# A graph layer on one core: gather tiles fetched row by row from SP and ACT, the last groups placed at once, and a place for every x chunk

## The chip, the cores and the metric

The kernel runs on one core of one Trainium2 chip. The time is device microseconds of that core, the median of three executions. One more execution was profiled, and all rows shown come from it. The engines are named as in the profile: PE (matmul; PEld loads its weights), DVE, ACT, POOL, and SP, which only issues transfers. A "q" behind a name (SPq, ACTq) marks what the engine's sequencer does, issuing a DMA among it.

## The reference

```python
h = jnp.maximum(_layernorm(x, axis=-1), 0.0)          # x: 12500 x 256, f32
agg = jax.ops.segment_sum(h[src], dst, num_segments=N) # 200000 edges, sorted by dst
z = (1.0 + eps_gin) * h + agg
t = jnp.dot(z, W1) + b1                                # 256 -> 512
t = jax.nn.relu(_batchnorm(t, g1, bt1))
conv_out = jnp.dot(t, W2) + b2                         # 512 -> 256
out = x + jax.nn.relu(_batchnorm(conv_out + h, g2, bt2))
```

The batch norms take mean and variance over all 12,500 nodes, so each of them is a barrier: nothing behind it can start before the last node is in.

## The kernel before

Edges are cut into 1,563 tiles of 128, and tiles into 131 groups of 12 (`GT`; the last group has 3). Nodes are cut into 25 chunks of 512 rows (the last has 212). One row of h or x is 256 f32, 1 KB.

**Gather loop** (lines 359 to 627). Its instructions stand in the order in which the program writes them; nothing is moved by the framework's scheduler. Iteration i of the loop does, for different groups:

- `gather(i + 4)`: an indirect DMA of POOL per tile (L473), which fetches 128 rows by their source numbers. The first 30 groups (`LEAD`) fetch rows of x and normalize them on ACT and DVE (`settle`); later ones fetch rows of `h_tab`, which the first 25 iterations write (`h_chunk`). Gathered tiles have five places, so `gather(i + 4)` needs `sums(i - 1)` done. Within a group the tiles are fetched from the last to the first.
- `edges(i + 1)` (L502, DVE) makes the 0/1 matrices, and `sums(i)` (L517, PE) multiplies the tiles with them, from the first tile to the last, into one PSUM tile `ps`.
- `hold(i - 2)` (L524, ACT) copies `ps` to `zs`; `put(i - 2)` (L535, PE) spreads it over the 256 columns that the group can reach; `add(i - 4)` (L546, DVE) adds it into the chunk `zc`, which `z_load` (L492, SP) fetched from `h_cols` and `z_scale` (L496, ACT) scaled.
- A chunk that has all its groups is multiplied by W1 in four slices, one slice per iteration: `slice_of` (L553, PE), then in the next iteration `take`: statistics on DVE (L564), a copy `ts` on ACT (L566) and its store to `t_tab`, issued by ACT (L567).

After the last group, the loop runs four more iterations with what is left, and all slices still queued are done there.

In every fifth group from 34 to 124 (`APART`), the first tile is not gathered by POOL. SP fetches its 128 rows one by one (`some_rows`): it loads 16 row numbers into registers (L412), then issues 16 DMAs of 1 KB (L418), two such batches per iteration, into the tile `one`, of which there are three. The semaphores of all these DMAs are the framework's, which it deals out in turn over all DMAs of SP and ACT.

**Second product** (lines 655 to 684). Per chunk: load `ti` from `t_tab` (three places) and `yT` from `h_cols` (25 places), norm and relu on ACT (L672), multiply by W2 on PE (L679), add and take statistics on DVE. From here on the framework's scheduler may move a DMA ahead of others on its queue.

**Output** (lines 691 to 715). Per chunk: norm and relu on ACT (L699), transposes on PE (L705), add the chunk of x on DVE (L710), and store (L331). The chunks of x are loaded by SP (`x_rows`, L333): ten into places of their own or into gather buffers that are done (`xin`, `lands`), six into `xmore`, which lies where `ti` was, and the last nine into places whose chunk has been stored.

Of the kernel before, what the change touches and what calls it, by code (L numbers as in the profile page):

```python
# [7 lines left out]
F32 = mybir.dt.float32  # L8
I32 = mybir.dt.int32
# [6 lines left out]
P = 128  # L16
R = 4
# [6 lines left out]
LOW = 8  # L24
APART = 5
BATCH = 16
XAHEAD = 10
XMORE = 6
# [3 lines left out]
GROUP = 4  # L32
GAHEAD = 3


@with_exitstack
def kernel(
# [37 lines left out]
    left = E - full_tiles * P  # L75
    NG = -(-NTILE // GT)
    STEP = -(-N * P * GT // E)
    WIDE = P + 2 * MARGIN
# [231 lines left out]
    def fast():  # L310
# [24 lines left out]
        with ExitStack() as fs:  # L335
# [8 lines left out]
            with ExitStack() as es:  # L344
# [21 lines left out]
                def settle(v, pairs, rows, to, tag):  # L366
# [16 lines left out]
                    for c in reversed(range(rows)):  # L383
# [3 lines left out]

                by_row = range(LEAD + 4, NG - 6, APART)
                rows_i = keep.tile([len(by_row), P], I32, name="rows_i")
                nc.scalar.dma_start(  # L390
                    rows_i,
                    bass.AP(
                        tensor=src.tensor, offset=src.offset + by_row[0] * GT * P,
                        ap=[[APART * GT * P, len(by_row)], [1, P]],
                    ),
                )
                rows_b = keep.tile([len(by_row), P], I32, name="rows_b")
                nc.vector.tensor_scalar(rows_b, rows_i, float(4 * D), None, op0=OP.mult)
                h_bytes = h_tab.rearrange("n d -> (n d)").bitcast(U8)
                single, pending = {}, []  # L400

                def begin_rows(k):
                    i = by_row[k]
                    single[i] = sel.tile([P, D], F32, name="one", bufs=3)
                    pending.extend((k, b) for b in range(0, P, BATCH))

                def some_rows(count):

                    for _ in range(min(count, len(pending))):
                        k, b = pending.pop(0)  # L410
                        to = single[by_row[k]]
                        _, at = nc.values_load_multi_w_load_instructions(  # L412
                            rows_b[k : k + 1, b : b + BATCH], engines=[mybir.EngineType.SP], min_val=0,
                            max_val=(N - 1) * 4 * D,
                            skip_runtime_bounds_check_because="node numbers are below N",
                        )
                        for q, v in enumerate(at):
                            nc.sync.dma_start(  # L418
                                to[b + q : b + q + 1, :].bitcast(U8),
                                h_bytes[bass.ds(v, 4 * D)].rearrange("(o e) -> o e", o=1),  # L420
                            )

                xts, hts, pcs = {}, {}, {}
# [43 lines left out]
                def gather(i):  # L467
                    t0, n = groups[i]
                    k = i % (AHEAD + 1)
                    ga = lands[k] if k < EARLY else (gat.tile([P, GT, D], F32, name="gt"),)  # L470
                    for t in reversed(range(t0 + (i in by_row), t0 + n)):
                        rows = left if t == full_tiles else P
                        nc.gpsimd.indirect_dma_start(  # L473
                            out=slot(ga, t - t0)[:rows], out_offset=None, in_=x if i < LEAD else h_tab,
                            in_offset=bass.IndirectOffsetOnAxis(ap=srcT[:rows, t : t + 1], axis=0),
                        )
                    gathered[i] = ga
# [31 lines left out]
                def sums(i):  # L509

                    t0, n = groups[i]
                    ga, oh = gathered.pop(i), ohs.pop(i)
                    alone = single.pop(i, None)
                    ps = ps_s.tile([P, D], F32, name="ps")
                    for j in range(n):
                        rows = left if t0 + j == full_tiles else P
                        nc.tensor.matmul(  # L517
                            ps, lhsT=oh[:rows, j, :], rhs=alone if alone is not None and j == 0 else slot(ga, j)[:rows], start=(j == 0), stop=(j == n - 1)
                        )
                    summed[i] = ps  # L520
# [62 lines left out]
                for c in range(NCH):  # L583
                    k = max(first(c) + 1, c + 2)
                    loads.setdefault(k, []).append(c)
                    scales.setdefault(max(first(c) + 3, c + 3), []).append(c)
                    assert c + 1 < k <= first(c) + 4 and c < LEAD - AHEAD
                added = whole = 0
                for i in range(NG + 4):
                    before = added  # L590
                    if i + AHEAD < NG:
                        gather(i + AHEAD)
                    if i + APART + 3 in by_row:
                        begin_rows(by_row.index(i + APART + 3))
                    some_rows(2)

                    late = 4 if i < NG else 3
                    while added <= min(i - late, NG - 1):
# [4 lines left out]
                    taken = []  # L603
                    if 0 <= i - 2 < NG:
                        spots(i - 2)
                        hold(i - 2)
                    if i + 1 < NG:
                        edges(i + 1)

                    if i < NCH:  # L610
                        h_chunk(i)
                    if i + 1 < min(LEAD, NG):
# [4 lines left out]
                    if i < NG:  # L617
                        sums(i)
# [3 lines left out]
                    if 0 <= i - 2 < NG:  # L622
                        put(i - 2)
                    for c in loads.get(i, ()):
                        z_load(c)
                    while whole < NCH and last(whole) < (before if i < NG else added):
                        queue += [(whole, f) for f in range(HC)]
                        whole += 1
                    if i < NG:
                        some = queue[:1]  # L630
                    else:
                        some = queue
                    queue = queue[len(some):]
                    if i < NG:
                        for c, f in some:
                            slice_of(c, f)
                        taken = some
                    else:
                        for c, f in some:
                            slice_of(c, f)  # L640
                            take(c, f)
                assert added == NG and whole == NCH and not queue and not taken and not zc, (queue, taken, list(zc))

# [5 lines left out]

            xin = fs.enter_context(tc.tile_pool(name="xin", bufs=XAHEAD - EARLY, reuse_waits="tile"))  # L650
            xrs = []

            def x_rows(g):
                if g < NCH:
                    if XAHEAD - EARLY <= g < XAHEAD:
                        xrs.append(lands[g - XAHEAD + EARLY][1])
                    else:
                        pool = xmore if XAHEAD <= g < XAHEAD + XMORE else xin
                        xrs.append(pool.tile([P, R, D], F32, name="xr"))
                    carry(nc.sync, xrs[g], x, g, store=False)  # L660


            with tc.tile_pool(name="tin", bufs=3, side="right", reuse_waits="tile") as tin, tc.tile_pool(name="ps_y", bufs=4, space=PSUM) as ps_y:

                for k, g in enumerate([*range(NCH - 2), NCH - 1, NCH - 2]):
                    n = chunks[g][1] * R
                    ti = tin.tile([P, HC, CH], F32, name="ti")
                    nc.sync.dma_start(ti[:, :, :n], t_tab[g, :, :, :n])
                    nc.sync.dma_start(yT[g], h_cols[g, :, :, :n])
                    tT = lands[k % EARLY][0].rearrange("p a d -> p (a d)").rearrange("p (f n) -> p f n", n=CH)  # L670
# [5 lines left out]
                    for d in range(DC):  # L676
# [289 lines left out]
```

## Time and profile before

| | |
|---|---|
| median of 3 runs | 2212.31 us (2211.7 to 2213.7) |
| profiled execution | 2212.03 us, of which the span from first to last instruction is 2210.0 us |
| mean granted TensorE clock | 0.817 |
| busy: PE, PEld, DVE, ACT, POOL | 1388.4, 1005.3, 716.0, 511.3, 1463.2 us |
| DMA | 349.80 MB, mean 158 GB/s |

The page cuts the span into 40 slices of 55 us and gives each engine's busy tenths in them. The granted clock is a share of full speed. A group of instructions has its line, its engine, what it writes and reads, a count, its busy time, the mean duration in ns, and the idle time of the engine before it with what ended that idle time ("issue" is time in which the engine waited for nothing that the profile shows). A row of the timeline has start, duration, engine, line, operation, tiles and count.

### The profile page before, as it was taken

Reading aid. Unit: us, or ns where it says so; the run is one execution under the profiler, and the core shown is the slowest. Engines: PE = TensorE matmul, PEld = TensorE weight load, DVE = VectorE, ACT = ScalarE, POOL = GpSimd, SP = SyncE. Lnnn points to the kernel's source line nnn. Section 1 sums busy time; section 2 is a strip of 40 time slices with the busy share of each in tenths; the row PEclk is TensorE's granted clock in tenths of the full one; section 3 lists DMA queues with packets and bytes.
Section 4 is the critical chain, followed back from the end, with each engine's and each line's share of the span. In section 5 each row is a group of like instructions: output and inputs, shape, how many; then the busy total and the mean of one; then the engine's idle time right before and its main releaser. Section 6 shows DMA issues by size and latency. Waiting matters only on the chain.

```text
span 2210.0 us, 20247 instructions
## 1 busy us (share of the span) xinstructions
PE 1388.4 (63%) x4874; PEld 1005.3 (45%) x4874; DVE 716.0 (32%) x1093; ACT 511.3 (23%) x963; POOL 1463.2 (66%) x1556
## 2 busy tenths in 40 slices
PE   3666676764654655754765566564466366689994
PEld 2455455553443543543544454443354254444443
DVE  5566666531211221220222122211123022234445
ACT  4666666530000000000000000000001001024445
POOL 7777777777777777777777777777777777700000
PEclk9777888887877877877878887786788687889998
DMA  6676777544444444444444444444444445448639
GB/s 195 210 229 220 237 243 236 168 130 116 135 128 129 118 131 130 124 130 121 126 136 127 116 135 131 131 116 127 131 122 134 123 122 148 137 152 329 231 112 314
DMA packets 161627, 349.80 MB, mean 158 GB/s; under 512 B 32234, under 2 KB 87033, under 8 KB 158427
## 3 DMA queue, kind: packets, MB, share of 16 engines
q0 software_dynamic: 74096, 202.41, 33.0%
q1 hardware_dynamic: 59088, 106.53, 14.4%
q10 hardware_dynamic: 28314, 39.48, 5.0%
q8 instruction: 41, 0.67, 0.1%
q14 instruction: 88, 0.71, 0.1%
HBM read 284.29 MB, written 64.00 MB: 158 GB/s over the span
## 4 chain that ended last, share of the span: by engine, by line
POOL 39%; issue 18%; PE 17%; DMA 8%; SPq 7%; ACT 7%; DVE 3%; ACTq 0%; DVEq 0%; POOLq 0%
POOL gt L473 24%; POOL gta L473 9%; PE py L679 8%; PE ps L517 5%; SPq L418 5%; POOL gtb L473 5%; DMA gt<-in_x_dram,srcT 3%; PE ph L553 2%; ACT gt L384 2%; SPq L412 1%; PE pz L535 1%; ACT yT L699 1%; DVE stg L373 1%; DMA t_tab<-ts 1%; DMA gta<-in_x_dram,srcT 1%
## 5 line engine op out<-in xcount | busy, mean ns | idle before, releaser
L473 POOL DMA_INDIRECT gt<-h_tab,srcT x701 | 662.6, 945 | 213.6 <-issue 212.1
L517 PE MATMUL ps<-gt,oh 128*128 128x256 f32 x1834 | 497.1, 436 | 185.6 <-DMA gt<-h_tab,srcT 104.3
L517 PEld LDWEIGHTS ps<-gt,oh 128*128 128x128 f32 x1834 | 407.0, 224 | 290.7 <-issue 110.1
L473 POOL DMA_INDIRECT gta<-h_tab,srcT x323 | 305.3, 945 | 98.5 <-issue 96.9
L546 DVE TENSOR_TENSOR zc<-pz,zc 128x512 f32<-128x512 f32 (+8 forms) x187 | 94.5, 520 | 770.2 <-ACT zc L496 710.8
L535 PE MATMUL pz<-at,zs 128*128 128x256 f32 x524 | 152.7, 418 | 286.4 <-ACT zs L524 286.4
L517 PE MATMUL ps<-gta,oh 128*128 128x256 f32 x838 | 241.7, 452 | 135.6 <-DMA gta<-h_tab,srcT 73.0
L517 PEld LDWEIGHTS ps<-gta,oh 128*128 128x128 f32 x838 | 192.7, 234 | 197.5 <-issue 91.2
L473 POOL DMA_INDIRECT gt<-in_x_dram,srcT x216 | 204.1, 945 | 65.8 <-issue 61.8
L535 PEld LDWEIGHTS pz<-at,zs 128*128 128x128 f32 x524 | 104.5, 207 | 308.7 <-ACT zs L524 295.3
L502 DVE TENSOR_TENSOR oh<-col,dstT 128x1536 f32<-128x1536 f32 x131 | 227.5, 1737 | 0.0
L553 PE MATMUL ph<-zc,w1s 128*128 128x512 f32 (+1 forms) x400 | 207.5, 649 | 11.6 <-DVE hc L461 10.9
L564 DVE BATCH_NORM_STATS2 st<-ph 128x6 f32<-128x512 f32 (+1 forms) x100 | 68.2, 682 | 452.0 <-PE ph L553 451.9
L566 ACT COPY ts<-ph 128x512 f32<-128x512 f32 (+1 forms) x100 | 57.4, 574 | 675.0 <-DVE st L564 675.0
L496 ACT ACTIVATE zc<-zc,gin 128x1024 f32<-128x1024 f32 (+1 forms) x25 | 28.1, 1124 | 672.4 <-DMA zc<-h_cols 672.4
L473 POOL DMA_INDIRECT gtb<-h_tab,srcT x160 | 151.2, 945 | 48.8 <-issue 47.8
L679 PE MATMUL py<-gta,w2s 128*128 128x512 f32 (+1 forms) x400 | 169.6, 587 | 3.7 <-ACT gta L672 3.7
L553 PEld LDWEIGHTS ph<-zc,w1s 128*128 128x128 f32 x400 | 85.9, 217 | 80.2 <-issue 56.2
L679 PEld LDWEIGHTS py<-gta,w2s 128*128 128x128 f32 x400 | 76.3, 191 | 96.5 <-issue 76.6
L384 ACT ACTIVATE gt<-gt,nbg,rsg 128x256 f32<-128x256 f32 x216 | 108.1, 586 | 9.0 <-DVE nbg L382 8.5
L517 PE MATMUL ps<-one,oh 128*128 128x256 f32 x38 | 17.4, 551 | 146.1 <-DMA one<-h_tab 146.1
L672 ACT ACTIVATE gta<-ti,of,sc 128x512 f32<-128x512 f32 (+1 forms) x100 | 79.6, 802 | 82.9 <-PE py L679 78.3
(100 smaller groups left out, 1052.6 us busy)
## 6 DMA issues: line engine op xcount, KB each, us to landing
one<-h_tab SPq DMA_DIRECT2D x2432, 1.0 KB
t_tab<-ts ACTq DMA_DIRECT2D x96, 256.0 KB
ti<-t_tab SPq DMA_DIRECT2D x24, 1024.0 KB
xt<-in_x_dram SPq DMA_DIRECT2D x24, 512.0 KB
h_tab<-ht ACTq DMA_DIRECT2D x24, 512.0 KB
h_cols<-hc SPq DMA_DIRECT2D x24, 512.0 KB
zc<-h_cols SPq DMA_DIRECT2D x24, 512.0 KB
yT<-h_cols SPq DMA_DIRECT2D x24, 512.0 KB
```

The lines of the kernel that those rows point to most:

```text
L384: nc.scalar.activation(slot(to, c), slot(v, c), AF.Relu, bias=nb[:, c : c + 1], scale=rs[:, c : c + 1])
L418: nc.sync.dma_start(to[b + q : b + q + 1, :].bitcast(U8), h_bytes[bass.ds(v, 4 * D)].rearrange("(o e) -> o e", o=1),)
L473: nc.gpsimd.indirect_dma_start(out=slot(ga, t - t0)[:rows], out_offset=None, in_=x if i < LEAD else h_tab, in_offset=bass.IndirectOffsetOn ...
L502: nc.vector.tensor_tensor(ohs[i][:, :n, :], col[:, :P].unsqueeze(1).to_broadcast([P, n, P]), dstT[:, t0 : t0 + n].unsqueeze(2).to_broadcas ...
L517: nc.tensor.matmul(ps, lhsT=oh[:rows, j, :], rhs=alone if alone is not None and j == 0 else slot(ga, j)[:rows], start=(j == 0), stop=(j == ...
L535: nc.tensor.matmul(pz[:, d, :], lhsT=zs[:, d * P : (d + 1) * P], rhs=at, start=True, stop=True)
L546: nc.vector.tensor_add(side, pz[:, :, a - lo : b - lo], side)
L553: nc.tensor.matmul(ph[:, :n], lhsT=w1s[:, d, f * P : (f + 1) * P], rhs=zc[c][:, d, :n], start=(d == 0), stop=(d == DC - 1),)
L564: nc.vector.bn_stats(st1[:, f, c, :], ph[:, :n])
L566: nc.scalar.copy(ts[:, :n], ph[:, :n])
L672: nc.scalar.activation(tT[:, f, :n], ti[:, f, :n], AF.Relu, bias=of1[:, f : f + 1], scale=sc1[:, f : f + 1],)
L679: nc.tensor.matmul(py[:, :n], lhsT=w2s[:, f, d * P : (d + 1) * P], rhs=tT[:, f, :n], start=(f == 0), stop=(f == HC - 1),)
```

## The change

- SP's rows now make up 26 tiles and ACT issues the rows of 19 more. A class `Fetcher` does it for both: of every 15 groups SP serves 4 (`SP_PACE`; tile 0 of the group), and of every 5 groups ACT serves 1 (`ACT_PACE`; tile 1). Row numbers are loaded into registers 32 at a time (`LOADS`). They are fetched for each tile by a small DMA of its own on SP in iterations 19 and 20.
- Each such tile has a semaphore allocated by the kernel. Its 128 DMAs add to it, the framework's semaphores leave them out, and PE waits for all of them before the matmul of that tile. In the group's sum these tiles come last.
- The last five groups (`CLOSE`) and what follows have a loop of their own: `hold`, `put` and `add` of a group stand right behind its sums, every finished chunk is multiplied by W1 at once, and the sums take the tiles in the order in which they were gathered.
- Every chunk of x has a place that no store must free: 8 in `xin`, 5 and the rest of the last chunk in buffers that the gather loop is done with (`lands`, `dstT`, `srcT`, `w1s`), loaded behind the third chunk of the second product; 6 in `xmore` and 5 in `lands` and `w2s`, loaded at its end.

```diff
-APART = 5
-BATCH = 16
-XAHEAD = 10
+LOADS = 32
+SP_PACE = (15, 4)
+ACT_PACE = (5, 1)
+XIN = 8
 XMORE = 6
+CLOSE = 5
...
+                class Fetcher:
+                    def __init__(self, eng, kind, pace, begin, end, slot, tag):
...
+                        while begin + 2 + -(-(count + 1) * over // self.per) < end:
+                            count += 1
+                        self.groups = [begin + 2 + -(-(k + 1) * over // self.per) for k in range(count)]
...
+                    def step(self, i):
+                        upto = min((i + 1 - self.begin) * P * self.per // self.over, len(self.groups) * P)
+                        upto -= upto % LOADS
+                        while self.sent < upto:
+                            k, b = divmod(self.sent, P)
+                            self.fetch(k, b, LOADS)
+                            self.sent += LOADS
+                    def fetch(self, k, b, n):
+                        g = self.groups[k]
+                        if b == 0:
+                            self.tiles[g] = sel.tile([P, D], F32, name="one_" + self.tag, bufs=3)
+                            self.sems[g] = tc.alloc_semaphore(f"rows_{self.tag}{k}")
                         _, at = nc.values_load_multi_w_load_instructions(
-                            rows_b[k : k + 1, b : b + BATCH], engines=[mybir.EngineType.SP], min_val=0,
+                            self.at[k : k + 1, b : b + n], engines=[self.kind], min_val=0,
...
                         for q, v in enumerate(at):
-                            nc.sync.dma_start(
-                                to[b + q : b + q + 1, :].bitcast(U8),
+                            d = self.eng.dma_start(
+                                self.tiles[g][b + q : b + q + 1, :].bitcast(U8),
                                 h_bytes[bass.ds(v, 4 * D)].rearrange("(o e) -> o e", o=1),
                             )
+                            d.then_inc(self.sems[g], 16)
+                            tc.no_tile_sem_insts.add(d.ins.name)
+                            tc.add_to_no_dep_group(f"{self.tag}{g}", d.ins)
+                    def use(self, g):
+                        wait = nc.tensor.wait_ge(self.sems.pop(g), 16 * P)
+                        tc.declare_fence(wait.ins, group=f"{self.tag}{g}")
+                        return self.tiles.pop(g)
+                fetchers = [
+                    Fetcher(nc.sync, mybir.EngineType.SP, SP_PACE, LEAD - AHEAD + 1, NG - 1, 0, "s"),
+                    Fetcher(nc.scalar, mybir.EngineType.Activation, ACT_PACE, LEAD - AHEAD + 1, NG - CLOSE, 1, "a"),
+                ]
...
-                    for j in range(n):
+                    order = list(range(n)) if i < NG - CLOSE else list(reversed(range(n)))
+                    own = alone(i)
+                    order.sort(key=lambda j: j in own)
+                    for j in order:
...
+                for i in range(NG - CLOSE, NG + 1):
+                    if i + AHEAD < NG:
+                        gather(i + AHEAD)
+                    fetchers[0].step(i)
...
+                    while near < i:
+                        hold(near)
+                        while added < near - 1:
+                            add(added)
+                            added += 1
+                        put(near)
+                        near += 1
+                    while added < near:
+                        add(added)
+                        added += 1
+                    while whole < NCH and last(whole) < added:
+                        queue += [(whole, f) for f in range(HC)]
+                        whole += 1
+                    for c, f in queue:
+                        slice_of(c, f)
+                        take(c, f)
+                    queue = []
                     if i < NG:
+                        sums(i)
...
-                for g in range(XAHEAD):
-                    x_rows(g)
+                behind = [lands[k][1] for k in range(EARLY)]
+                behind += [rows_in(dstT), rows_in(srcT.bitcast(F32)), rows_in(w1s.rearrange("p a b -> p (a b)"))]
+                with tc.issue_after(begun):
+                    x_rows([(g, xin.tile([P, R, D], F32, name="xr")) for g in range(XIN)])
+                    x_rows(enumerate(behind, XIN))
+                    x_rows([(NCH - 1, rows_in(dstT, R * D, len(parts[NCH - 1])))])
...
-                for g in range(XAHEAD, XAHEAD + XMORE):
-                    x_rows(g)
+                got = len(xrs) - 1
+                x_rows([(g, xmore.tile([P, R, D], F32, name="xr")) for g in range(got, got + XMORE)])
+                last = [lands[k][0][:, c : c + R, :] for k in reversed(range(EARLY)) for c in range(0, LOW, R)]
+                last += [rows_in(w2s.rearrange("p a b -> p (a b)"))]
+                x_rows(enumerate(last, got + XMORE))
...
                     carry(nc.sync, xt, out, g, store=True)
-                    if g >= 3:
-                        x_rows(g - 3 + XAHEAD + XMORE)
```

More of the change, by code (lines that the diff above doesn't have):

```diff
@@ L625, in fast @@
                         z_load(c)
-                    while whole < NCH and last(whole) < (before if i < NG else added):
+                    while last(whole) < before:
                         queue += [(whole, f) for f in range(HC)]
                         whole += 1
-                    if i < NG:
[L630 to L633, printed above, removed]
-                    if i < NG:
[L635 to L641, printed above, removed]
@@ L642, in fast @@
[L642 removed]
+                    taken = queue[:1]
+                    queue = queue[1:]
+                    for c, f in taken:
+                        slice_of(c, f)
+                near = NG - CLOSE - 2
+                for c, f in taken:
+                    take(c, f)
+                for i in range(near, NG - CLOSE):
+                    spots(i)
+                for i in range(NG - CLOSE, NG + 1):
+                    if i + AHEAD < NG:
+                        gather(i + AHEAD)
+                    fetchers[0].step(i)
+                    if i < NG:
+                        spots(i)
+                    if i + 1 < NG:
+                        edges(i + 1)
+                    for c in scales.get(i, ()):
+                        z_scale(c)
+                    while near < i:
[12 more added lines that the diff above has]
+                    for c, f in queue:
+                        slice_of(c, f)
+                        take(c, f)
+                    queue = []
+                    if i < NG:
+                        sums(i)
@@ L644, in fast @@
+                assert added == near == NG and whole == NCH and not zc, list(zc)
             sc1, of1 = norm(keep, st1, mv1, HC, g1c, bt1c, b1c, "1")
```

101 lines of the change are left out of this document (49 added, 52 removed).

## The prediction

> **What bounds the kernel now.** I read the page first, then the busy times by stretch, then the waits, and last single rows of the instructions by line, of the chain and of the timeline. From the page:
>
> ```profile
> span 2210.0 us, 20247 instructions
> ...
> POOL 7777777777777777777777777777777777700000
> ...
> L473 POOL DMA_INDIRECT gt<-h_tab,srcT x701 | 662.6, 945 | 213.6 <-issue 212.1
> ```
>
> POOL works at one level until about 1935 us and then stops. The row of L473 says at what pace: (662.6 + 213.6) / 701 = 1.250 us for each indirect gather, 0.945 busy and 0.305 of its own issue. Of the 213.6 us idle before these gathers, 212.1 are that issue: no buffer, no late engine and no transfer holds POOL up. The stretches (us; then busy us and count of PE, PEld, DVE, ACT, POOL; TensorE clock, DMA share, GB/s) show the stages:
>
> ```profile
> 1000.00:1500.00 500.00, 290.37 (x1026) 219.54 (x1024) 106.26 (x138) 33.21 (x64) 378.10 (x401) 0.80 0.45 127
> ...
> 1935.00:1977.00 42.00, 32.38 (x91) 20.14 (x92) 13.86 (x30) 8.47 (x18) 1.51 (x2) 0.86 0.40 137
> 1977.00:2147.00 170.00, 169.43 (x400) 76.13 (x399) 67.96 (x100) 78.50 (x99) 0.00 (x0) 0.99 0.65 230
> 2147.00:2210.00 63.00, 28.29 (x196) 22.96 (x196) 32.48 (x35) 35.18 (x51) 0.00 (x0) 0.78 0.83 282
> ```
>
> So there are four: the gather loop, bound by POOL's count of gathers while ACT is busy 7% and DVE 21%; a tail of 40 us after the last gather; the second product, where PE works through; and the output, where PE, DVE and ACT are half idle and the DMA engines are not.
>
> **Gather loop: what goes.** Before, 19 of the 1,563 tiles are fetched by SP; after, 26 by SP and 19 by ACT. The pace formula gives that: SP's tiles serve groups 33, 37, 41 and on to 127, ACT's 34, 39 and on to 124. POOL thus issues 26 gathers fewer: 26 x 1.250 = **32.5 us**, all of it on the path. Its last gather ends at 1936.8 us now (below), and at 1904.3 then.
>
> **What the sequencers take on.** The two issue rows and the loads of addresses (min/median/max ns), and two loads of the chain that are four batches apart:
>
> ```profile
> L412 SPq TENSOR_LOAD <-rows_b x152: 1160/1248/1509, 423.8 to 1859.0; - x152
> L418 SPq DMA_DIRECT2D one<-h_tab x2432: 221/228/323, 425.5 to 1868.0; - x188
> L931 SPq TENSOR_LOAD <-flag x1: 476/476/476, 25.5 to 25.5; - x1
> L567 ACTq DMA_DIRECT2D t_tab<-ts x100: 325/326/357, 200.8 to 1974.8; - x100
> ...
> 537.33 1.23 SPq L412
> ...
> 563.77 1.24 SPq L412
> ```
>
> Four batches of 16 rows took 563.77 - 537.33 = 26.44 us, 6.61 each; less one load, 5.37 for 16 rows: 0.336 us per row, with the register move and now and then an instruction fetch. A load of 32 addresses is not in the trace. One address cost 0.476 and 16 cost 1.248; the straight line gives 2.07, and two loads of 16 give 2.50. I take 2.07. A tile is then 128 x 0.336 + 4 x 2.07 = 51.3 us (53.0 at the other end).
>
> SP starts at 423.8 us. Its last tile serves group 127, behind which POOL issues 12 + 12 + 3 = 27 gathers, so the tile is wanted at about 1904.3 - 27 x 1.25 = 1870. That leaves (1870 - 424) / 26 = 55.6 us a tile: SP keeps up, with 8% to spare, provided that it doesn't wait. Today it does:
>
> ```profile
> SPq L418 <- DMA t_tab<-ts: 422.8, 70, 23.6
> ...
> PE ps L517 <- DMA one<-h_tab: 146.1, 10, 24.1
> ```
>
> A row DMA of SP waits for a store that ACT issues; the DMAs share a few of the framework's semaphores in turn, so a row must wait until the store which had that semaphore has landed. With a semaphore of its own per tile, a row takes none of these, and the 422.8 us go. What is late next on SP is only the reuse of three buffers, which is what the pace is for. Behind a waiting row stand h_cols loads (`z_load`), on which ACT's scaling and DVE's adds depend; they come earlier, not later. PE's 146.1 us of waiting for rows cost POOL nothing now: group i + 4 only needs group i - 1 summed, some three groups (43 us) of cover. I count them at zero.
>
> ACT has no rows in the trace. In five groups, 5 x 11.55 x 1.25 = 72.2 us, it must issue one tile: 51.3 us at SP's price, and 51.3 + 128 x 0.098 = 63.8 if a row costs as much more as ACT's own large store (326 ns against 228). Its work of now is 33.21 us in 500, 1.0 per group, and a 0.33 us issue: 6.5. Sum 57.8 to 70.3, below 72.2 at both ends; I take the lower, since it is the same kind of DMA. Queued behind its 32 rows (12.8 us) are the `ts` copies, `zs` copies and `zc` scaling, for which PE's `put` and DVE's `add` wait; they come a group late at most, inside the same cover. The 45 address loads on SP (45 x 0.336 = 15 us, groups 19 and 20), two small DVE operations and 45 waits on PE lie beside the gathers of those groups, which wait for none of it; without that cover they would cost the 15 us once.
>
> **Early placing.** The end of the loop, from the chain and the timeline:
>
> ```profile
> 1932.16 3.02 DMA gt<-h_tab,srcT
> ...
> 1935.87 0.95 POOL L473 DMA_INDIRECT gta<-h_tab,srcT  x1 [0.31 <-issue]
> ...
> 1953.96 10.44 PE L553 MATMUL ph<-zc,w1s 128*128 128x512 f32 x20
> ...
> 1966.15 0.37 ACT L524 COPY zs<-ps 128x256 f32<-128x256 f32 x1 [0.40 <-ACT ts L566]
> ...
> 1976.80 0.70 PE L679 MATMUL py<-gta,w2s 128*128 128x512 f32 x1 [3.71 <-ACT gta L672]
> ```
>
> POOL ends at 1936.8 and the second product begins at 1976.8: 40.0 us. Between lie sums that begin with the tile gathered last, a backlog of slices (20 matmuls, 10.4 us), and group 130's placing. After, group i is placed right behind its sums, finished chunks are multiplied at once, and the last five groups sum the first-gathered tile first. What must follow POOL's end is the landing, 3.0; the last sums, about 2 (PE comes out of chunk 23's slices and group 129 at about that time); and the stretch from `zs` to `py`, 1976.80 - 1966.15 = 10.7. That is 15.7: **24.3 us saved**, at best 26. If chunk 23's slices still stand in the way, 15 us come back and 10 are saved. I take 24.3, since PE is busy 58% before it.
>
> **Places for all x chunks.**
>
> ```profile
> 1976.80 169.64 PE py L679 x400
> ...
> 2137.63 3.96 SPq L333 DMA_DIRECT2D xr<-in_x_dram  x6
> ...
> 2149.90 34.89 ACT L699 ACTIVATE yT<-yT,of,sc 128x512 f32<-128x512 f32 x50 [0.82 <-DVE of L287]
> ...
> 2185.26 1.23 DVE L710 TENSOR_TENSOR xr<-po,xr 128x1024 f32<-128x1024 f32 x1 [0.50 <-DMA out_dram<-xr]
> 2193.35 1.93 SPq L333 DMA_DIRECT2D xr<-in_x_dram  x2
> 2195.38 7.53 SPq L331 DMA_DIRECT2D out_dram<-xr  x7
> ...
> 2160.00:2190.00 30.00, 19.97 (x147) 15.64 (x147) 22.81 (x19) 24.78 (x36) 0.00 (x0) 0.99 1.08 369
> ```
>
> Today nine x chunks are loaded between the stores, each into a place that a store must free; the last is asked for at 2193.35, when ACT has been done for 8.6 us. At 369 GB/s the engines are full. After, 14 chunks come during the second product (230 GB/s, so there is room) and 11 at its end, 5.6 MB in the 17 us from 2137.6 that pass before the first output is ready. The stores alone, 12.8 MB / 369 GB/s = 34.7 us, fit ACT's 34.9. The last add then ends near 2186.5, and with the 7.1 us that now lie between the last store's issue (2202.9) and the end, plus a microsecond of backlog: 2194.6, **15.4 us saved** (8 with a backlog of another 7.5, 18 with none and a shorter drain).
>
> **The sum.** The profiled execution took 2212.03 us (span 2210.0 and 2.0 around it), the median of three is 2212.31, so nothing is to be shifted. 2212.0 - 32.5 - 24.3 - 15.4 = 2139.8; I say **2140**. The second product keeps its 169.6 us.
>
> **Rivals.**
>
> *Two issuers hold each other up* (slower). If SP's and ACT's DMAs are made by one unit that takes 0.228 us each, a row's pitch is 0.456, SP's tile 66.7 us and its last one ready at 424 + 26 x 66.7 = 2158 instead of 1870: 288 us late, 2428. It decides from 55.6 us a tile; the gain is gone at 58.3, a pitch of 0.39. Against it:
>
> ```profile
> 1360.85 1.52 SPq L418 DMA_DIRECT2D one<-h_tab  x5
> ...
> 1361.39 0.33 ACTq L567 DMA_DIRECT2D t_tab<-ts  x1
> ```
>
> Five rows took 1.52 us, their usual 0.32 each, with an ACT issue in their midst. [...] Chance 6%.
>
> *One DMA engine is full* (slower).
>
> ```profile
> q0 software_dynamic: 19202, 52.46, 38.5%
> q10 hardware_dynamic: 3600, 6.56, 3.6%
> q1 hardware_dynamic: 2546, 4.01, 2.8%
> ...
> one<-h_tab SPq DMA_DIRECT2D x844, 1.0 KB
> ...
> zc<-h_cols SPq DMA_DIRECT2D x6, 512.0 KB
> ```
>
> Between 1000 and 1500 us, SP's queue used 2.8% of 16 engines x 500 us = 224 us for 844 rows and six loads of h_cols, 3.1 MB. The latter at the price of ACT's stores (288 us for 6.56 MB) is 138, which leaves 0.10 us a row; at most it is 0.27. If all 5,760 rows went to one engine in 1,446 us, that is 40% of it (at most 107%), beside 38.5% of gathers and some 6%: 84%. It decides above 0.14 us a row; at 0.27 the loop would stretch by half, far over 2,700 us. [...] No view here names the engine. Chance 4%.
>
> *x loads stand ahead of t loads.* Thirteen whole chunks and a rest, 7.0 MB, at 369 GB/s are 19 us; two filled `ti` buffers cover 2 x 6.8. PE starts the second product 5 to 10 us short: 2148. For it: all fourteen are released at the third chunk. Against: SP serves earlier lines of the program first. 10%.
>
> *The ends give half*: 10 from placing, 8 from the places: 2161. 13%.
>
> *The change doesn't free SP*: rows still wait for t_tab. The 423 us make the last tile ready at 424 + 1334 + 423 = 2181, 311 late: 2451. 2%.
>
> **The numbers.** Forecast 65%. The range reaches from 2133 (the best ends, 26 and 18, give 2135.5; the second product at a clock of 1.0 instead of 0.99 takes 1.7 less) to 2166 (the halved ends, 2161, and 5 us of late t loads). It holds the forecast and the two rivals on its side, 88%; I leave the rest of that for terms I have mis-sized. A measurement here can tell about 0.2% from no change, 4 us. Faster by more: the 88%; the 12% of the three slower cases, of which a mild form (a pitch of 0.37 to 0.39) still leaves a gain, are split into 0.01 faster, 0.01 same and 0.10 slower.
>
> **What would show it.** Right: POOL x1530 with its last gather near 1904 and a 1.25 us pitch; SP's waits for t_tab gone; `py` beginning near 1920; no x load later than 5 us after the last `py`; span near 2138. Wrong: gathers that wait for PE's sums, PE waiting tens of us for `one_s` or `one_a`, a row pitch above 0.39, or gaps in `py`.

## The result, and the profile after

The changed kernel takes **2147.01 us** (median of four runs, 2145.12 to 2148.0) against 2212.28 us before: a ratio of 0.9703, 95% interval 0.9686 to 0.972. The profiled execution took 2145.12 us, 1.9 below the median, with a span of 2143.3 us; the span before was 2210.0, so 66.7 us are to be found. From the page of after:

```profile
span 2143.3 us, 26894 instructions
...
POOL 7777777777777777777777777777777777740000
...
L510 POOL DMA_INDIRECT gt<-h_tab,srcT x681 | 643.9, 945 | 207.7 <-issue 199.8
```

POOL still works at one level and now stops near 1905 us instead of 1937 (a slice is 53.6 us long here and was 55.3 before, so the digits alone do not show it). Its pace is what it was: (643.9 + 207.7) / 681 = 1.250 us per gather. The stretches of after (us; busy us and count of PE, PEld, DVE, ACT, POOL; TensorE clock, DMA share, GB/s):

```profile
1000.00:1500.00 500.00, 321.32 (x1076) 243.49 (x1074) 113.06 (x146) 34.14 (x66) 378.09 (x400) 0.82 0.48 131
...
1905.00:1921.30 16.30, 9.20 (x31) 5.92 (x30) 6.26 (x16) 3.21 (x9) 0.00 (x0) 0.90 0.37 132
1921.30:2091.00 169.70, 169.63 (x400) 76.39 (x400) 67.42 (x99) 78.80 (x99) 0.00 (x0) 0.99 0.69 246
2091.00:2144.00 53.00, 27.90 (x196) 22.68 (x196) 32.88 (x35) 35.17 (x51) 0.00 (x0) 0.87 0.93 305
```

POOL issues 400 gathers in 500 us, as before (401), but PE, DVE and ACT do more work in the same time: 1,076 matmuls instead of 1,026. The tail is 16.4 us, not 40; the second product is unchanged; the output is 53 us with the DMA engines at 93%.

The issue rows (min/median/max ns) and, from the waits of SP, its two largest:

```profile
L430 SPq TENSOR_LOAD <-at_s x104: 2056/2172/2932, 424.5 to 1761.7; - x104
L430 ACTq TENSOR_LOAD <-at_a x76: 2145/2591/3001, 461.1 to 1789.4; - x76
L436 SPq DMA_DIRECT2D one_s<-h_tab x3328: 227/228/514, 426.9 to 1774.2; - x196
L436 ACTq DMA_DIRECT2D one_a<-h_tab x2432: 234/235/547, 463.4 to 1802.6; - x188
```

```profile
SPq L497 <- DVE hc L496: 186.2, 23, 17.4
SPq L734 <- DMA t_tab<-ts: 118.2, 4, 84.3
```

No row waits any more: L436 is not among SP's waits. The wait for `t_tab` that is left stands at L734, which loads `yT` from `h_cols` for the second product. These loads do not read `t_tab`, but still use the framework's semaphores, as they did before (70.6 us at L669). A row costs 228 ns to issue on SP and 235 on ACT. The end of the loop, from the timeline and the chain:

```profile
1903.98 0.94 POOL L510 DMA_INDIRECT gta<-h_tab,srcT  x1 [0.30 <-issue]
...
1910.59 0.37 ACT L564 COPY zs<-ps 128x256 f32<-128x256 f32 x1 [5.13 <-PE ps L557]
```

```profile
1903.98 5.83 DMA gta<-h_tab,srcT
...
1921.33 169.65 PE py L746 x400
```

POOL's last gather ends at 1904.9 and the second product begins at 1921.3.

### The profile page after: what moved, and what is told of

Its sections match the earlier page's. It is cut to its first block, busy times and chain, and to the rows that moved or that the text cites. A ratio compares the mean times of both kernels' runs of the same rounds, so it can differ in the third digit from the quotient of the medians.

```text
span 2143.3 us, 26894 instructions
## 1 busy us (share of the span) xinstructions
PE 1445.9 (67%) x4874; PEld 1039.4 (48%) x4874; DVE 716.7 (33%) x1094; ACT 511.2 (24%) x963; POOL 1438.9 (67%) x1530
## 3 DMA queue, kind: packets, MB, share of 16 engines
q14 instruction: 140, 1.15, 0.2%
## 4 chain that ended last, share of the span: by engine, by line
POOL 40%; PE 18%; issue 17%; DMA 13%; ACT 7%; DVE 4%; ACTq 0%; DVEq 0%; SPq 0%; POOLq 0%
POOL gt L510 26%; POOL gta L510 8%; PE py L746 8%; PE ps L557 7%; POOL gtb L510 5%; DMA gta<-h_tab,srcT 5%; DMA gt<-h_tab,srcT 4%; ACT gt L387 2%; DMA gt<-in_x_dram,srcT 2%; PE ph L593 2%; DVE stg L376 2%; ACT yT L774 2%; PE pz L575 1%; ACT gta L387 1%; DVE oh L539 1%
## 5 line engine op out<-in xcount | busy, mean ns | idle before, releaser
L510 POOL DMA_INDIRECT gt<-h_tab,srcT x681 | 643.9, 945 | 207.7 <-issue 199.8
L557 PE MATMUL ps<-gt,oh 128*128 128x256 f32 x1794 | 524.6, 461 | 332.7 <-DMA gt<-h_tab,srcT 252.9
L557 PEld LDWEIGHTS ps<-gt,oh 128*128 128x128 f32 x1794 | 418.2, 238 | 463.8 <-issue 240.4
L557 PE MATMUL ps<-gta,oh 128*128 128x256 f32 x826 | 289.0, 525 | 275.2 <-DMA gta<-h_tab,srcT 202.2
L557 PEld LDWEIGHTS ps<-gta,oh 128*128 128x128 f32 x826 | 221.9, 275 | 356.9 <-issue 156.6
L593 PE MATMUL ph<-zc,w1s 128*128 128x512 f32 (+1 forms) x400 | 192.4, 608 | 22.3 <-DVE hc L496 21.4
L575 PE MATMUL pz<-at,zs 128*128 128x256 f32 x524 | 138.6, 388 | 21.4 <-ACT zs L564 17.1
L564 ACT COPY zs<-ps 128x256 f32<-128x256 f32 x131 | 48.1, 371 | 327.7 <-issue 262.6
L593 PEld LDWEIGHTS ph<-zc,w1s 128*128 128x128 f32 x400 | 77.4, 197 | 83.3 <-issue 49.0
L557 PE MATMUL ps<-gtb,oh 128*128 128x256 f32 x416 | 98.3, 379 | 0.0
```

Of the source, the lines that this page charges most:

```text
L510: nc.gpsimd.indirect_dma_start(out=slot(ga, t - t0)[:rows], out_offset=None, in_=x if i < LEAD else h_tab, in_offset=bass.IndirectOffsetOn ...
L557: nc.tensor.matmul(ps, lhsT=oh[:rows, j, :], rhs=fetched[:rows], start=(j == order[0]), stop=(j == order[-1]))
L564: nc.scalar.copy(zss[i], summed.pop(i))
L575: nc.tensor.matmul(pz[:, d, :], lhsT=zs[:, d * P : (d + 1) * P], rhs=at, start=True, stop=True)
L593: nc.tensor.matmul(ph[:, :n], lhsT=w1s[:, d, f * P : (f + 1) * P], rhs=zc[c][:, d, :n], start=(d == 0), stop=(d == DC - 1),)
```

## The experiments

All times are medians; each ratio compares a kernel with runs of the kernel before on the same chip. The differences from the changed kernel are differences of medians that were not always taken on one chip; the kernel before had medians from 2211.8 to 2213.3 us there.

**1. SP alone.** ACT's fetcher and its step are taken out, so 26 tiles go by row and POOL has 19 gathers more than in the changed kernel.

```diff
-    Fetcher(nc.scalar, mybir.EngineType.Activation, ACT_PACE, LEAD - AHEAD + 1, NG - CLOSE, 1, "a"),
...
-    if i >= fetchers[1].begin:
-        fetchers[1].step(i)
```

> The changed kernel without ACT's 19 tiles; POOL gathers them again. If POOL's count of gathers sets the loop: 19 x 1.25 = 23.8 us more than the changed kernel's 2147.0, so 2171, with the same pitch of 1.250 on POOL. If the two issuers crowd each other on the way to the DMA engines, part of what ACT's tiles brought was lost again, and taking them away costs less, 10 us or so: 2157, with SP's row pitch below the 0.326 us that it has beside ACT.

2170.75 us, ratio 0.9806 (0.979 to 0.9822): 23.7 us over the changed kernel, where 19 gathers are 19 x 1.25 = 23.75. POOL's last gather ended at 1928.4, 23.5 later than in the changed kernel. That the medians agree to 0.1 us is luck, since the runs reach from 2165.0 to 2172.5. SP's pitch from row to row was 0.325 us alone and 0.326 beside ACT (1,233 and 1,236 rows between 1000 and 1500 us), so the two issuers do not hold each other up. What the second issuer saves is here worth 23.7 us, because POOL's count of gathers, at 1.250 us each, is what bounds the loop. Whether a second issuer also brings bandwidth no run here tests.

**2. The loop's end of before.** Tiles fetched as in the changed kernel, but placing, slices and order of sums in the last groups as before.

```diff
-    order = list(range(n)) if i < NG - CLOSE else list(reversed(range(n)))
+    order = list(range(n))
...
-    for i in range(NG - CLOSE):
+    for i in range(NG + 4):
```

> The changed kernel with the loop end of before (one slice per iteration, four more iterations after the last group, sums from the first tile). If the late backlog and the late sums are what the new end saves: POOL's end to the first py goes from 16.4 back to about 40 us, 23.6 more, 2171. If most of the 24 us came of the fewer gathers (PE being less behind), under 12 more: 2159 or less.

2170.35 us, 0.9814 (0.9798 to 0.983): 23.3 us over the changed kernel. POOL ended at 1905.0, as there, and the chain has the second product 40.3 us later:

```profile
1945.23 169.65 PE py L726 x400
```

**3. The x places of before.** Ten chunks ahead, and then a load whenever a store has freed a place.

```diff
-XIN = 8
+XAHEAD = 10
...
+    if g >= 3:
+        x_rows(g - 3 + XAHEAD + XMORE)
```

> The changed kernel with the x places of before (nine chunks loaded into places that a store frees). The traces give 63.6 us before and 52.3 us after from the last py to the end: 11.3 more, 2158. If the second product also pays for the x loads that the change brings into it, less than 11: 2155 or below. If the places were worth the 15.4 us of the prediction and something else at the end ate 4: 2162.

2155.5 us, 0.9749 (0.9733 to 0.9765): 8.5 us over the changed kernel. From its last `py` to the end pass 62.1 us, against 52.3. Chain, SP's timeline and one stretch of it:

```profile
1919.53 169.48 PE py L745 x400
```

```profile
2135.26 0.82 SPq L336 DMA_DIRECT2D xr<-in_x_dram  x2
```

```profile
2105.00:2130.00 25.00, 17.85 (x132) 13.99 (x131) 20.76 (x17) 22.35 (x33) 0.00 (x0) 1.00 1.09 382
```

The late loads are back (one at 2135), and the output is 9.8 us longer. Its second product began 1.8 us earlier than the changed kernel's (1921.33), though POOL's last gather ended at the same time (1904.95). The x loads of the changed kernel cannot have delayed its `py`, since the first of them goes out at 1986.4. What differs is PE's pace between POOL's end and `py`. In the profiles of kernels with this same loop end the stretch took 14.6 us here and 15.5 in experiment 8, where the last group's four `pz` matmuls took 1.15 and 1.13 us; 16.4 in the changed kernel (1.47 us, at a granted TensorE clock of 0.90); 18.3 in experiment 6 (2.07, at 0.69); and 19.5 in experiment 1 (2.09). No run sets this clock on purpose, so that it is the cause is likely, not shown. Loads and stores together move 382 GB/s here.

**4. The framework's semaphores on the rows.** All else as in the changed kernel.

```diff
-    self.sems[g] = tc.alloc_semaphore(f"rows_{self.tag}{k}")
...
-    d.then_inc(self.sems[g], 16)
-    tc.no_tile_sem_insts.add(d.ins.name)
-    tc.add_to_no_dep_group(f"{self.tag}{g}", d.ins)
...
-    wait = nc.tensor.wait_ge(self.sems.pop(g), 16 * P)
-    tc.declare_fence(wait.ins, group=f"{self.tag}{g}")
```

> The changed kernel, but all row DMAs of SP and ACT use the framework's semaphores again, dealt out in turn. If the 423 us that SP's rows waited for t_tab stores came of these shared semaphores: SP's last tile is ready near 424 + 26 x 51.6 + 423 = 2189 instead of 1870 and the kernel takes 2400 us or more, with PE waiting for one_s. If the waiting was slack that SP had anyway, the time stays near 2147.

2513.4 us, 1.137 (1.1351 to 1.1389): 366 us over the changed kernel. From its waits:

```profile
ACT ts L600 <- DMA one_a<-h_tab: 448.3, 28, 19.1
ACT ts L600 <- DMA one_s<-h_tab: 418.1, 26, 18.7
...
PE pz L569 <- ACT zs L558: 743.4, 78, 32.4
POOL gt L504 <- PE ps L551: 168.3, 25, 21.5
```

I had expected PE to wait for late rows, and it did, but only for 123.5 us. SP's own rows waited 437 us at L435, and the larger part went another way: ACT stood in its own queue for rows to land, 866 us at the `ts` copies, so its `zs` copies came late, PE waited for those, and POOL's gathers in the end for PE. With the shared semaphores one queue waited here for another's transfers: ACT 418.1 us for SP's rows.

**5. Own semaphores in the kernel before**, on its 19 tiles, which now come last in their sums.

```diff
+    d.then_inc(sems[by_row[k]], 16)
+    tc.no_tile_sem_insts.add(d.ins.name)
+    tc.add_to_no_dep_group(f"rows{by_row[k]}", d.ins)
```

> The kernel before with its 19 tiles on SP, and only a semaphore of its own for each (and its matmul last in the sum). SP's wait for t_tab stores should go from 423 us to nearly none. If POOL's count sets the loop, the time stays 2212 within 4 us. If those waits cost something by themselves, 10 us or more come off.

2211.42 us over ten runs, 0.9997 (0.9988 to 1.0006). The 422.8 us of waiting for `t_tab` are gone from SP's rows, which now wait for their three buffers instead (`z_load`, at L496, still waits 62.5 us for `t_tab`):

```profile
SPq L419 <- PEq L525: 165.8, 13, 15.9
SPq L419 <- PE ps L527: 72.5, 13, 6.3
```

SP was early enough with 19 tiles, so freeing it alone brings nothing. With 45 tiles on two queues the same edit is worth the 366 us of experiment 4.

**6. Without the late x loads.** Chunks 13 to 23 are stored without x: their loads are left out, and a copy stands for the add.

```diff
-    x_rows(enumerate(last, got + XMORE))
+    xrs.update(enumerate(last, got + XMORE))
...
+    if got <= g < NCH - 1:
+        nc.vector.tensor_copy(xt[:rows, c0:c1, :], po[:rows, c0:c1, :])
```

> The changed kernel without the x loads at the end of the second product: chunks 13 to 23 are stored without x added (a copy stands for the add). If the output stage is 5 us longer than predicted because stores alone move at 340 GB/s and not at the 369 of loads and stores mixed: nothing changes but a microsecond, 2145 to 2147, and the DMA rate between the first store and the end stays near 340. If it is longer because the eleven late loads are still in the way of the stores: 5 us less, 2142, and the rate rises to 369 or more.

2142.66 us, 0.9682 (0.9667 to 0.9697), 4.3 us less than the changed kernel; the intervals overlap. The time is the one expected if late loads were in the way, but the rate is the one expected if stores set the end. The output in stretches:

```profile
2105.00:2115.00 10.00, 7.65 (x56) 6.00 (x56) 8.88 (x9) 10.00 (x16) 0.00 (x0) 1.00 1.01 340
2115.00:2125.00 10.00, 7.76 (x57) 6.11 (x58) 8.69 (x8) 10.00 (x15) 0.00 (x0) 1.00 1.04 339
```

With no load left beside them the stores move 340 GB/s at a DMA share of 1.0. Stores alone were slower here than loads and stores together (382 in experiment 3). From the last `py` to the end pass 51.6 us, against 52.3 in the changed kernel, so in the profiles the late loads cost 0.7 us. The profiled execution was the slowest of the four (2146.47; the others took 2141.1 to 2143.5), and no profile shows where the rest of the 4.3 us lies.

**7. The late x loads in another order**, the first two of the six in `xmore` last.

```diff
+    x_rows(more[2:] + more[:2])
```

> The changed kernel with the six xmore loads issued in the order in which their places come free (four of them some 7 to 14 us earlier). If stores alone set the end: within 1 us of 2147.0. If late loads do: 2 to 4 us less.

2147.0 us, 0.9703 (0.969 to 0.9716): no difference, so the order of these loads is not what ends the output. Whether their presence costs more than the 0.7 us of experiment 6's profile stays open.

**8. Three tiles more by row** (27 on SP, 21 on ACT), with the order of 7.

```diff
-SP_PACE = (15, 4)
-ACT_PACE = (5, 1)
+SP_PACE = (11, 3)
+ACT_PACE = (9, 2)
```

> As x_order, and SP fetches 3 tiles in 11 groups instead of 4 in 15 (27 tiles), ACT 2 in 9 instead of 1 in 5 (21). Three gathers fewer on POOL: 3.75 us less than x_order, 2143. SP then needs 52 us a tile of 52.8 there are, ACT 59.5 of 64.8; if either is really full, PE waits for one_s or one_a and the time is above 2147.

2170.49 us, 0.9809 (0.9795 to 0.9823): 23.5 us slower than 45 tiles, a miss. Its POOL timeline, waits and one stretch:

```profile
641.17 0.94 POOL L510 DMA_INDIRECT gt<-h_tab,srcT  x1 [1.02 <-DMA gta<-h_tab,srcT]
...
645.23 0.95 POOL L510 DMA_INDIRECT gt<-h_tab,srcT  x1 [0.62 <-DMA gt<-h_tab,srcT]
```

```profile
POOL gt L510 <- DMA gt<-h_tab,srcT: 17.6, 37, 2.4
```

```profile
470.00:1000.00 530.00, 342.87 (x1136) 255.77 (x1134) 116.56 (x152) 35.70 (x70) 391.47 (x416) 0.82 0.47 128
```

In that stretch the changed kernel issued 425 gathers, this one 416. The idle time before a gather, 0.30 us throughout the changed kernel, is over 0.4 before 47 gathers here, 24.2 us in all beyond the 0.305. (The profiled execution took 2164.81, the lowest of the five.) PE does not wait for the rows; where the view names a releaser, it is mostly another gather's landing. So the transfers, not an issuer, seem to hold POOL up here, which no experiment shows by itself; experiments 11 and 12 say more about when. No version with the whole output tried here beats the changed kernel.

**9. The same with half a row.** Each row DMA moves 512 bytes; the other half of these tiles' columns repeats the first.

```diff
-    h_bytes[bass.ds(v, 4 * D)].rearrange("(o e) -> o e", o=1),
+    h_bytes[bass.ds(v, 2 * D)].rearrange("(o e) -> o e", o=1),
```

> The kernel with 27 SP tiles and 21 ACT tiles again, with each row DMA moving only the first half of the row (512 B; the other half of these tiles' columns gets the same values). The count of DMAs, their issue and their semaphore writes stay. If the stalls on POOL come of the time that the rows' bytes take on the DMA engine (or engines) that carry them: that time halves, the stalls are gone, 2143. If they come of the count of DMAs: 53 stalls of 24 us in all stay, 2165 to 2174.

2159.63 us, 0.9765 (0.9748 to 0.9783), between the two expectations. 36 gathers had a longer idle time, 17.6 us in all:

```profile
POOL gt L510 <- DMA gt<-h_tab,srcT: 12.2, 27, 1.4
```

Bytes are part of it, since 6.6 of the 24.2 us went with half of them; the count of rows may be the rest, which is not shown.

**10. Each row in four pieces of 256 bytes**, with the paces of 8. The question is whether the stalls come of rows that all go through one full engine; that four pieces go to more engines than a whole row does is an assumption that no run shows.

```diff
+SPREAD = 4
...
-    h_bytes[bass.ds(v, 4 * D)].rearrange("(o e) -> o e", o=1),
+    h_bytes[bass.ds(v, 4 * D)].rearrange("(o k e) -> o k e", o=1, k=SPREAD),
```

> The kernel with 27 SP tiles and 21 ACT tiles (it took 2170, with 24 us of short stalls on POOL that no wait of the program explains), and each row of 1 KB now moved as four pieces of 256 B, so that the copy's outer dimension is 4. [...] If they come of the number of small transfers, of memory, or of the two issuers: stalls stay or grow, 2170 or more.

3503.34 us, 1.583 (1.5803 to 1.5856). It does not answer the question, since the issue of such a row took 583 ns on SP, against 228 for a whole row in the changed kernel:

```profile
L437 SPq DMA_DIRECT2D one_s<-h_tab x3456: 3/583/1062, 428.9 to 3219.4; - x192
```

SP and ACT could not keep up and became the bound. It does show that a row pitch far above the prediction's 0.39 us, here from the issue alone (0.583 us), stretches the whole loop.

**11 and 12. Too many tiles on one issuer**: 30 tiles on SP, and 28 on ACT, with the other as in the changed kernel.

```diff
-SP_PACE = (15, 4)
+SP_PACE = (10, 3)
```

> The changed kernel with 3 SP tiles in 10 groups instead of 4 in 15: 30 tiles, 48 us for each where SP's rows and loads take 52. If SP's time per tile decides (55.6 us was the limit at 26 tiles): the last tile is ready near 424 + 30 x 52 = 1984 and wanted near 1896, 88 late; four gathers fewer give 5 back: 2230, with PE waiting for one_s. If SP has slack that the sum does not see: 2142.

```diff
-ACT_PACE = (5, 1)
+ACT_PACE = (10, 3)
```

> The changed kernel with 3 ACT tiles in 10 groups instead of 1 in 5: 28 tiles. ACT needs 54 us for a tile and 1.3 for each group, 58.3 in 3.33 groups that take POOL 47.6: 10.7 us over, 28 times, less the three groups of cover. If ACT's queue decides: 2147 - 11 + 300 - 43, about 2390, PE waiting for zs and POOL for PE. If rows on ACT only delay what nobody waits for: 2136.

2239.65 us (1.0127, 1.0097 to 1.0156) and 2359.3 us (1.0667, 1.0637 to 1.0698). The waits of the first, and then of the second:

```profile
PE ps L557 <- PEq L446: 98.8, 11, 22.5
...
PE pz L575 <- ACT zs L564: 342.8, 53, 32.2
```

```profile
PE pz L575 <- ACT zs L564: 691.0, 99, 19.4
POOL gt L510 <- PE ps L557: 158.2, 22, 13.4
```

A tile every 3.33 groups is one in 48.1 us. SP needs 128 x 0.326 + 4 x 2.17 = 50.4, and ACT 128 x 0.334 + 4 x 2.59 = 53.1 and its own work, so both fall behind. SP's timeline and the chain of the first, then the chain of the second, show the end:

```profile
1957.33 24.03 SPq L436 DMA_DIRECT2D one_s<-h_tab  x64
```

```profile
2014.86 170.59 PE py L746 x400
```

```profile
2134.44 169.36 PE py L746 x400
```

SP's last row goes out at 1981 instead of 1774. PE stands at L446 for the tiles' rows, and longer for `zs`: SP also issues the loads of `zc`, and ACT waited 250.7 us for them, where it had no such wait in the changed kernel. The second product begins 93.5 us later than there, which is the whole difference (92.6). With ACT it begins 213 us later (212.3 in the medians), by another path: behind a load and 32 rows on ACT stand `zs` copies that every group needs, so PE waits for `zs` and POOL's gathers for PE. That the harm is larger on ACT was expected, though 31 us too large; on SP the expectation was 10 too small.

The two also bear on the stalls of experiment 8. POOL's waits, of the first and then of the second:

```profile
POOL gt L510 <- issue: 263.3, 863, 0.3
POOL gtb L510 <- PE ps L557: 29.1, 5, 7.3
```

```profile
POOL gt L510 <- DMA gt<-h_tab,srcT: 26.1, 42, 2.2
```

With 30 tiles on SP and 19 on ACT, 49 in all, POOL was held up beyond its 0.3 us of issue only five times, each time by PE's sums and never by a landing. With 28 on ACT the waits for landings are back, up to 2.2 us. So it is not the number of tiles: the stalls came with 21 and 28 tiles on ACT and not with 30 on SP. The 30 bring no more rows at a time, though, because SP issued row after row already in the changed kernel (1,236 rows between 1000 and 1500 us; 1,234 here).

## Why the prediction was right

The forecast was 2140 with a range from 2133 to 2166; the median is 2147; the span was to be near 2138 and is 2143.3. Step by step:

| Step | Predicted, us | Profile of after, us | Undone alone, us |
|---|---|---|---|
| last gather ends (26 x 1.250 earlier) | 1904.3, saves 32.5 | 1904.9, saves 31.9 | 23.7 for ACT's 19 |
| end of the gathers to `py` | 15.7, saves 24.3 | 16.4, saves 23.6 | 23.3 |
| last `py` to the end | saves 15.4 | 52.3, saves 11.3 | 8.5 |

The savings in the profile add up to 66.8, which is the spans' difference of 66.7 but for rounding.

**Gather loop: right.** POOL has 1,530 instructions and its 1.250 us, with no idle time before a gather beyond its issue.

**What the sequencers take on: right, from a straight line.** A load of 32 addresses was estimated at 2.07 us and measured 2.17 on SP; on ACT it was 2.59, above the other end of 2.50. A row took 0.326 from start to start (0.336 predicted) and 0.334 on ACT. SP's last row went out at 1774, wanted at 1870. The forecast of 57.8 us per tile and five groups for ACT holds: 53.1 and some 6.5 of its own work are 59.6, below 72.2.

**Rows free of `t_tab`: right, and the cover was right too.** Experiment 5 shows that the 422.8 us cost nothing in the kernel before, experiment 4 that the change needs them gone. The rival that the change does not free SP had 2451; the kernel in which it does not took 2513, and through ACT rather than through late tiles.

**Early placing: right, by terms that were off both ways.** The last gather landed 5.83 us after its start, 4.9 after its end, where I had 3.0. The sums then took 0.8, not 2, and from `zs` to `py` were 10.74 (10.65 predicted). Together 16.4. That the two errors, of 1.9 and 1.2 us, nearly cancel is luck, and so is part of the closeness: the same stretch took 14.6 to 19.5 us in the other kernels with this end (experiment 3), and the sum had no term for that. No slice of chunk 23 stood in the way.

**Places for all x chunks: mechanism right, size off.** The mis-sized term is the stores' rate. I priced 12.8 MB at 369 GB/s, which I had read from a stretch in which loads run beside stores. After the change the stretch has only stores, and from 2105 on it shows

```profile
2105.00:2130.00 25.00, 19.51 (x145) 15.18 (x142) 21.65 (x19) 24.31 (x36) 0.00 (x0) 1.00 1.03 340
```

12.8 MB at 340 GB/s are 37.6 us, 2.9 more than the 34.7 of the sum, and these no longer fit under ACT's 35.17: the last add's stores find a backlog. The timeline has the last add:

```profile
2130.62 0.74 DVE L785 TENSOR_TENSOR dstT<-po,dstT 128x256 f32<-128x256 f32 x2
```

It ends 40.4 us after the last `py`, where the sum had 40.1. From there to the end pass 11.9 us, where the sum had 8.1: nearly the whole 4.1 us lies in this last term. SP's rows of the timeline:

```profile
2092.72 1.33 SPq L336 DMA_DIRECT2D w2s<-in_x_dram  x1
2099.05 9.55 SPq L334 DMA_DIRECT2D out_dram<-xr  x8
...
2131.76 2.95 SPq L334 DMA_DIRECT2D out_dram<-dstT  x2
```

The last x load is asked for 1.7 us after the last `py`, within the 5 that I had set. The last store is issued at 2134.7 and the end comes 8.6 us later, against 7.1 before. Experiment 6 has the same 340 with no x load in flight at all, so it is the stores' own rate, and there too 11.2 us pass from the last add to the end. So of the 3.8 us that this term was short, 3.1 remain without any late load, about the 2.9 of the rate. The other 0.7 goes with the late loads in the profiles: eleven chunks are 5.8 MB, not the prediction's 5.6, they moved at 352 GB/s between 2085 and 2099, and by an estimate from these two figures they took 16.4 us and were not quite done when the first store went out at 2099. What the loads cost outside the profiles stays open (experiment 6).

**Rivals.** *Two issuers hold each other up* falls with the pitch of 0.325 alone and 0.326 together. *x loads ahead of t loads* has no gap to show: `py` takes 169.65 us, as before, and the first x load goes out 65 us after it began. *The ends give half* falls by the table.

*One DMA engine is full* did not come about, but its neighbourhood did. From the DMA queues between 1000 and 1500 us:

```profile
q1 hardware_dynamic: 3471, 4.94, 3.4%
...
one_s<-h_tab SPq DMA_DIRECT2D x1236, 1.0 KB
```

SP's queue has 392 rows more than before and uses 0.6% of 16 x 500 us, 48 us, more. Of its 0.93 MB more, 0.53 are another load of `h_cols`, 23 us at the price of ACT's stores in the prediction. That leaves 25 us, some 0.06 us a row (0.04 to 0.08 with the rounding), below the 0.10 that I used. The packet records of the trace give it directly: between 1000 and 1500 us, 1,231 rows of SP and 886 of ACT took 0.072 us each on the mean, and a packet of 4 bytes that goes with each 0.010, together 0.08. They also bear on whether it is one engine. Rows of the two queues overlap for only 0.4 us in all these 500; with ACT's rows shifted in time against SP's by up to 60 us, they would overlap for 10.6 on the mean. So the rows of both issuers went one after another, as through one engine. If it is one, it was, by an estimate from these records, busy with rows 34% of the time, and with the gathers' mean share of 39.7% and the other packets' 6.3% about 80%, near the 84% of the prediction. On the mean that is not full; yet with 27 and 21 tiles POOL stalls in short pieces. Bytes matter to this (experiment 9). Whether the pieces come from moments at which several rows and a gather meet on that engine stays open: no view here names the engine, and the kernel meant to spread the rows fell to their issue cost of 583 ns.

## What to carry to other kernels

Where, as on POOL here, nothing else holds an issuing engine up, its time is a count by a pitch, 1.250 us a gather: the 26 gathers that other sequencers took over were worth 31.9 us, and this holds up to the point where a sequencer, or the transfers themselves, no longer keep up. Both points were near: 30 tiles instead of 26 made SP late, and 27 and 21 instead of 26 and 19 brought the stalls. Price a stretch by a row in which the same mix runs: stores alone moved 340 GB/s here, loads and stores together 369 to 382. A queue's waits that cost nothing today (422.8 us here) can be what a heavier load on that queue fails on (366 us in experiment 4), so look at whose transfers a shared semaphore makes it wait for.

## What the runs showed of the hardware

- Stores alone moved 340 GB/s at a full DMA share, x loads alone 352 (2085 to 2099 us), loads and stores together 369 to 382 (before, and experiment 3).
- The load of 32 addresses took 2.17 us on SP and 2.59 on ACT; the issue of a row DMA 228 and 235 ns; of the same row as four pieces 583 ns on SP.
- Single rows beside the gathers cost POOL nothing with 26 tiles on SP and 19 on ACT, nor by landings with 30 and 19; with 27 and 21 they cost it 24.2 us in short stalls, and half the bytes per row took 6.6 of these back.
- Rows issued by SP and by ACT hardly ever moved at the same time: 0.4 us of overlap where shifted ones would have 10.6.
